# A hand-written order for the SAGE loop of a four-layer graph network, and three steps for one in the last endings

## The chip, the cores and the metric

The kernel runs on one core of a Trainium2 chip. The metric is the device time of one execution in microseconds (us); the time of a kernel is the median of its runs. Engines are named as the profile names them: PE (TensorE matmul), PEld (TensorE weight load), ACT (ScalarE), DVE (VectorE), POOL (GpSimd), SP (SyncE).

## The reference

A graph of N = 3327 nodes with an int32 adjacency matrix, 512 features a node, four layers in a row. Each layer normalises its input over the features and adds its result to that input.

```
h = layernorm(x) ;  layer 0: graph attention, 8 heads of 64; then batch norm over the nodes, relu, + x  -> x1
h = layernorm(x1);  layer 1 (SAGE): mean of the neighbours' rows of relu(h);
                    own = relu(h) @ W_self + b_self ; nb = mean @ W_nb + b_nb ;
                    relu([own, nb] @ W_comb + b_comb) + x1                       -> x2
h = relu(layernorm(x2)); layer 2: graph attention, 8 heads of 64; elu, + x2      -> x3
h = relu(layernorm(x3)); layer 3: the same with its own weights; elu, + x3       -> out
```

Graph attention projects h to W h, scores each edge (i, j) by a leaky relu of a sum of one number for i and one for j, takes the softmax over the neighbours j of i, and sums the rows of W h with it.

## The kernel before, in words

Nodes are padded to 3328, 26 blocks of 128. Edges are sparse, so the kernel works on lists. For each group of 64 destination nodes (52 groups, two to a block) it holds a list of source nodes, cut into chunks of 128; the groups have 22, 15, 13, 12, 11, 10, 9, 9, 9 chunks, then four times 8, six times 7, eleven times 6, twenty-one times 5, and 4: 359 in all. A chunk's 128 source rows are fetched by one indirect DMA that POOL issues (L1106).

**Attention** (`attend`, layers 0, 2 and 3) runs over units of three chunks: DVE makes weights (L1207, L1214), PE sums rows with them (facc, L1228). When a group's sum is complete, a generator `ending(g)` finishes it in steps (sums, rd, eight products into the block, then exp, add and store), one step for each unit that follows. `later()` advances every open ending by one step and then calls `tick()`, which does one step of some other work: the folding of SAGE's weights during layer 0, the projection of layer 3 during layer 2. Attention's loop already stands inside `tc.manual_schedule` for PE, DVE and ACT: these engines take their instructions in the order in which the program's text gives them. Outside such a block the Tile scheduler chooses the order.

**SAGE** (layer 1, in `sparse`) needs no weights from DVE. Before its loop, `own` adds each block's own part into `bn_y` (s_ps, L1387). The loop then goes over parts. A part is up to two chunks (SUNIT) of each of a block's two groups; `load(i)` casts their masks on ACT (z_mask, L1444) and has POOL gather their rows (z_rows, L1106). Both have eight tile buffers (SROWS), and parts are loaded two ahead (SAHEAD). PE adds a chunk into sage_acc (L1463), in pairs, one chunk of each group. Ahead of each pair stands `tick()`, which advances each open `ending(b, acc)` by a step and then the next layer's projection by a step. The ending of a block is, step by step: s_ag (ACT, L1402: sum times 1/degree), a_ps and aT (PE transposes L1406, ACT copy L1408), n_ps (PE, L1412, and the load of fsage_x), s_o (DVE, L1417 and L1418, and the store of x2), after which the block goes to the projection.

**The projection of the next layer** (`Following`) takes each block of x2 through ten steps or so. In `norm`: ln_j, ln_s, rs_g, rs_y on ACT (sums for the mean and the variance); a DVE step of the reciprocal root; ln_s and ln_h on ACT (L795, L796). In `rest`: p_ps and hT (PE transposes L803, ACT L806); p_sd (PE, L810) and three ACT operations on it (v_row L814 and L815, s_col L817); p_wh (PE, L823); r_full, r_half and the eight products v_row (ACT, L827) and the table's store; p_tr (PE, L831); r_row and its store (ACT, L834). One `tick` does up to two steps of the oldest block in `rest`, then one step of each block in `norm`.

```
def tick(self):
    for _ in range(min(2, len(self.ready))):
        while self.ready and next(self.ready[0]) is None:
            self.ready.pop(0)
    for g in list(self.early):
        hx = next(g)
        ...
```

After the loop the open endings are run down, `proj.drain()` finishes the projection, and a row of the mean (mean_ps, L699) closes the table; layer 2's gathers wait for it.

Of the kernel before, what the change touches and what calls it, by code (L numbers as in the profile page):

```python
# [23 lines left out]
F32 = mybir.dt.float32  # L24
# [9 lines left out]
ET = mybir.EngineType  # L34
# [4 lines left out]
P = 128  # L39
H = 8  # L40
F = 64
D = H * F
# [8 lines left out]
GB = 64  # L51
CAPS = (22, 15, 13, 12, 11, 10, 9, 9, 9) + 4 * (8,) + 6 * (7,) + 11 * (6,) + 21 * (5,) + (4,)
# [8 lines left out]
SAHEAD = 2  # L61
# [1016 lines left out]
def sparse(ctx: ExitStack, tc: tile.TileContext, t: dict, out: bass.AP, WA, ls, cs, idx, rdeg, first):  # L1078
# [5 lines left out]
    nc = tc.nc  # L1084
# [4 lines left out]
    PG = P // GB  # L1089

    def used(c):
        return min(P, N - c * P)
# [12 lines left out]
    def gather(dst, src, k):  # L1105
        nc.gpsimd.indirect_dma_start(  # L1106
            out=dst, out_offset=None, in_=src[:, :], in_offset=bass.IndirectOffsetOnAxis(ap=idx[:, k : k + 1], axis=0)
        )


    def attend(layer, table, r_dram, finish, tick=lambda: None, home=None):
# [11 lines left out]
        with tc.tile_pool(name=f"fatt{layer}", bufs=2) as ap, tc.tile_pool(  # L1123
            name=f"facc_ps{layer}", bufs=2, space=PSUM
        ) as aps, tc.manual_schedule(engines={ET.PE, ET.DVE, ET.Activation}):
            rows, rrs, rbs, accs, ends = {}, {}, {}, {}, []
# [42 lines left out]
                    del hps[b]  # L1169
                    yield from fin  # L1170

            def later():
                for e in list(ends):
                    if next(e, 0) == 0:
                        ends.remove(e)
                tick()

            for g in range(2):
# [23 lines left out]
            for i, (g, k0, n, begins, stops) in enumerate(units):  # L1202
# [11 lines left out]
                nc.vector.tensor_tensor(wt[:, :n], mx[:, :n], mk.unsqueeze(2).to_broadcast(full), ALU.mult)  # L1214
                load(i + 1)
                later()
                if begins:
                    fetch(g + 2)
                    acc = aps.tile([P, BANK], F32, name="facc", tag="acc")
# [3 lines left out]
                for k in range(n):  # L1223
                    f, l = begins and k == 0, stops and k == n - 1
                    for q in range(hq):
                        for v in range(PG):
# [5 lines left out]
                                start=(f and q == 0),  # L1232
                                stop=(l and q == hq - 1),
                            )
                if stops:
                    ends.append(ending(g))
            while ends:
                later()

    def following(lx, layer, wl, W, pb=1):  # L1240

        table = dram.tile([NP, ROW], I32, name=f"table{layer}")
        r_dram = dram.tile([ls.G, 2, H, GB], F32, name=f"r_dram{layer}")
        pp = lx.enter_context(tc.tile_pool(name=f"fproj{layer}", bufs=1))
        pps = lx.enter_context(tc.tile_pool(name=f"fproj_ps{layer}", bufs=1, space=PSUM))
        return Following(tc, cs, N, wl, W, WA, table, r_dram, pp, pps, pb)
# [24 lines left out]
    with ExitStack() as mx:  # L1271
# [48 lines left out]
        with tc.tile_pool(name="beside", bufs=1) as wp, tc.tile_pool(name="beside_ps", bufs=1, space=PSUM) as wps:  # L1320
            bg = beside(wp, wps)

            def done(c, hp, pool):
                yield
                whole.append(c)
                yield

            attend(0, *first, done, lambda: next(bg, None), y)
            for _ in bg:
                pass  # L1330
# [4 lines left out]
        proj = following(mx, 2, 1, t["L2_gnn_W"], 2)  # L1335
        gp = mx.enter_context(tc.tile_pool(name="fsage", bufs=2))
        gps = mx.enter_context(tc.tile_pool(name="fsage_ps", bufs=2, space=PSUM))
        two = [P, 2, D]
        with tc.tile_pool(name="fbn", bufs=1) as bp:
            var_ps = gps.tile([P, D], F32, name="var_ps", tag="n_ps")  # L1340
            for c in range(0, NB, 2):
# [3 lines left out]
                for i in range(2):  # L1345
                    k = used(c + i)
# [51 lines left out]
        ends = []  # L1398

        def ending(b, acc):  # L1400
            ag = gp.tile([P, D], F32, name="s_ag", tag="s_ag")
            nc.scalar.mul(ag, acc, rdeg[:, b : b + 1])  # L1402
            yield
            tp = gps.tile([P, KC, P], F32, name="a_ps", tag="a_ps")
            for kc in range(KC):
                nc.tensor.transpose(tp[:, kc, :], ag[:, kc * P : (kc + 1) * P], cs["ident"])  # L1406
            aT = gp.tile([P, KC, P], F32, name="aT", tag="aT")
            nc.scalar.copy(aT, tp)  # L1408
            yield
            ps = gps.tile([P, D], F32, name="n_ps", tag="n_ps")  # L1410
            for kc in range(KC):
                nc.tensor.matmul(ps, aT[:, kc, :], Wx[:, 1, kc, :], start=(kc == 0), stop=(kc == KC - 1))  # L1412
            xr = gp.tile([P, D], F32, name="fsage_x", tag="sage_x", bufs=3)
            nc.sync.dma_start(xr, x1[b * P : (b + 1) * P, :])
            yield
            o = gp.tile([P, D], F32, name="s_o", tag="s_o", bufs=3)
            nc.vector.tensor_tensor(o, ps, y[:, b, :], ALU.add)  # L1417
            nc.vector.scalar_tensor_tensor(o, o, 0.0, xr, ALU.max, ALU.add)  # L1418
            nc.sync.dma_start(x2[b * P : (b + 1) * P, :], o)
            proj.begin(b, o)  # L1420

        def tick():
            for e in list(ends):
                if next(e, 0) == 0:
                    ends.remove(e)
            proj.tick()


        parts = []
# [3 lines left out]
        loaded = {}  # L1433

        def load(i):
            if i >= len(parts):
                return
            zs = loaded[i] = []
            for u, kn in enumerate(parts[i][1]):
                if kn is not None:  # L1440
                    k0, n = kn
                    zt = gp.tile([P, SUNIT, D], F32, name="z_rows", tag="z_rows", bufs=SROWS)
                    mf = gp.tile([P, SUNIT, GB], F32, name="z_mask", tag="z_mask", bufs=SROWS)
                    nc.scalar.copy(mf[:, :n, :], mask[:, k0 : k0 + n, :])  # L1444
                    for k in range(n):
                        gather(zt[:, k, :], h_dram, k0 + k)
                        zs.append((k, u, k0 + k, mf[:, k, :], zt[:, k, :]))
            zs.sort(key=lambda x: x[:2])

        for i in range(SAHEAD):  # L1450
            load(i)
        for i, (b, _, begins, stops) in enumerate(parts):
            load(i + SAHEAD)
            if begins:
                acc = gps.tile([P, D], F32, name="sage_acc", tag="sage_acc")
            at = -1
            for r, u, k, m, z in loaded.pop(i):
                if r != at:
                    at = r
                    tick()  # L1460
                g = b * PG + u
                f, l = k == ls.first[g], k == ls.first[g] + CAPS[g] - 1
                nc.tensor.matmul(acc[u * GB : (u + 1) * GB, :], m, z, start=f, stop=l)  # L1463
            if stops:
                ends.append(ending(b, acc))
        while ends:
            tick()
        proj.drain()


    with ExitStack() as l3:
        at2 = proj
        proj = following(l3, 3, 2, t["L3_gnn_W"])
        attend(2, at2.table, at2.r_dram, elu_into(x2, x3, proj.begin), proj.tick)
        proj.drain()
    attend(3, proj.table, proj.r_dram, elu_into(x3, out))


def gnn_stack(tc: tile.TileContext, t: dict, out: bass.AP):
    with ExitStack() as ctx:  # L1480

        tc.nc.scalar.preload_act_table_set("natural_log_exp_and_others")
        N, NP = out.shape[0], t["x"].shape[0]
        ls = Lists(NP)
        cs = constants(ctx, tc, N)
        kp = ctx.enter_context(tc.tile_pool(name="first", bufs=1))
        ldram = ctx.enter_context(tc.tile_pool(name="first_dram", bufs=1, space=DRAM))

        table = ldram.tile([NP, ROW + NP // WB // 2], I32, name="table0")
        r_dram = ldram.tile([ls.G, 2, H, GB], F32, name="r_dram0")  # L1490
        idx = kp.tile([P, ls.n], I32, name="idx")
        rdeg = kp.tile([P, NP // P], F32, name="rdeg")
        with tc.tile_pool(name="wa1", bufs=1) as wp:
            prods = Products(tc, t, kp, wp)
            WA, ok = prods.WA, prods.ok
            with tc.tile_pool(name="fproj0", bufs=1) as pp, tc.tile_pool(name="fproj_ps0", bufs=1, space=PSUM) as pps:
                p = Projection(tc, cs, N, 0, t["x"], t["L0_gnn_W"], WA, table, r_dram, pp, pps, hb=1)
                lists(tc, t, ls, cs, N, prods, table, p, idx, rdeg)
        small = tc.nc.values_load(ok[0:1, 0:1], min_val=0, max_val=1, skip_runtime_bounds_check_because="a product of comparisons, 0 or 1")
        with tc.If(small > 0) as branch:  # L1500
            sparse(tc, t, out, WA, ls, cs, idx, rdeg, (table, r_dram))
        with branch.Else():
            general(tc, t, out)
# [60 lines left out]
```

## Time and profile before

| | us |
|---|---|
| median of 3 runs | 2963.6 |
| lowest and highest run | 2959.35, 2970.7 |
| the profiled execution, its own time | 2969.83 |
| its span in the profile | 2967.7 |
| PE, DVE, POOL, ACT busy in the span | 2177.8, 1813.4, 1384.6, 1069.6 |
| SAGE's first gather, first sage_acc, last sage_acc | 1036.8, 1044.3, 1640.3 |
| layer 2's first gather | 1671.4 |

The profile shows one execution. Times on its axis run from the span's start. Busy time is what an engine's records cover; a share of busy time over the whole span mixes stages with different limits, so the SAGE stage (some 630 us, a fifth of the span) is read by itself, from stretches of 74 us, each a fortieth of the span. The mean granted PE clock of the whole execution was 0.788 of full speed.

### The profile page before, as it was taken

The page shows a single profiled execution, that of the slowest core. Times are in us where ns is not written, and L with a number is a line of the kernel's source. Part 1 is how long each engine was busy: PE and PEld are TensorE (multiplying, and loading weights), DVE is VectorE, ACT ScalarE, POOL GpSimd, SP SyncE. Part 2 cuts the span into 40 slices and gives each one's busy share as a digit, 9 for nine tenths or more (in the row PEclk, how much of TensorE's full clock was granted, in tenths as well). Part 3 has the DMA queues.
Part 4 walks back from the last instruction along what each step waited for, and adds up shares of the span by engine and source line. Part 5 has one row for each costly group of instructions (what it writes and reads, how often), then busy time and mean ns, then how long its engine had stood idle before and what let it go on. Part 6 is the DMA issues. An engine that isn't in the chain of part 4 may idle for free.

```text
span 2967.7 us, 54270 instructions
## 1 busy us (share of the span) xinstructions
PE 2177.8 (73%) x21344; PEld 1372.4 (46%) x21344; DVE 1813.4 (61%) x2208; ACT 1069.6 (36%) x4013; POOL 1384.6 (47%) x1482
## 2 busy tenths in 40 slices
PE   2677577877675985888999567878777657677775
PEld 1444344555552431333333355655555346556664
DVE  8878487878776800011111377778667267888886
ACT  1233022323334412344455213555666501222333
POOL 1000365666550056656555365555444066666653
PEclk9778798867778997889999777877777766775655
DMA  7771477777662746666666466777565066677774
GB/s 280 279 263 56 161 233 231 252 210 213 200 200 77 249 142 194 192 203 209 198 199 189 131 184 186 202 199 195 169 177 165 31 192 190 194 199 198 205 203 127
DMA packets 188820, 562.09 MB, mean 189 GB/s; under 512 B 37780, under 2 KB 42320, under 8 KB 185230
## 3 DMA queue, kind: packets, MB, share of 16 engines
q0 software_dynamic: 115456, 404.86, 47.4%
q1 hardware_dynamic: 73102, 153.68, 14.7%
q8 instruction: 171, 2.80, 0.4%
q14 instruction: 91, 0.75, 0.1%
HBM read 498.74 MB, written 59.68 MB: 188 GB/s over the span
## 4 chain that ended last, share of the span: by engine, by line
PE 57%; issue 15%; ACT 8%; another core or an unknown queue 4%; DVE 3%; DMA 2%; POOL 0%; SPq 0%; DVEq 0%; ACTq 0%; POOLq 0%
PE facc L1228 29%; PE p_wh L823 7%; PE sage_acc L1463 5%; PE n_ps L1412 3%; PE r_bc L1139 3%; PE p_sd L810 2%; PE s_ps L1387 2%; ACT v_row L827 2%; PE bmean_ps L1315 1%; ACT fhp L1166 1%; PE fwx_ps L1305 1%; DVE mx L1207 1%; PE p_ps L803 1%; ACT hT L806 1%
## 5 line engine op out<-in xcount | busy, mean ns | idle before, releaser
L1106 POOL DMA_INDIRECT rows<-table,idx x1077 | 1025.3, 952 | 882.4 <-PE facc L1228 378.4
L1228 PE MATMUL facc<-rows,wgt 128*64 128x65 f32 x17232 | 982.1, 268 | 411.2 <-issue 399.1
L1228 PEld LDWEIGHTS facc<-rows,wgt 128*64 128x64 f32 x17232 | 829.8, 176 | 631.3 <-issue 588.1
L1207 DVE TENSOR_TENSOR mx<-r_bc,rows 128x1536 f32<-128x1536 f32 (+1 forms) x405 | 639.6, 1579 | 157.8 <-PE facc L1228 71.4
L1214 DVE TENSOR_TENSOR wgt<-mx,mask 128x1536 f32<-128x1536 f32 (+1 forms) x405 | 638.3, 1576 | 158.5 <-PE facc L1228 81.7
L1106 POOL DMA_INDIRECT z_rows<-h_dram,idx x359 | 340.2, 948 | 387.8 <-ACT hT L1384 140.2
L1166 ACT ACTIVATE fhp<-sums,rd 64x64 f32<-64x64 f32 x832 | 219.8, 334 | 137.5 <-DVE rd L1160 71.4
L1463 PE MATMUL sage_acc<-z_rows,z_mask 128*64 128x512 f32 x718 | 229.0, 655 | 9.6 <-DMA z_rows<-h_dram,idx 8.9
L823 PE MATMUL p_wh<-fWt,hT 128*128 128x512 f32 x416 | 227.1, 693 | 1.4 <-ACT s_col L817 1.4
L1156 ACT COPY sums<-facc 128x260 f32<-128x260 f32 x156 | 57.9, 371 | 402.6 <-PE facc L1228 366.3
L820 DVE TENSOR_SCALAR s_col<-s_col 128x8 f32<-128x8 f32 x52 | 9.9, 190 | 303.3 <-ACT s_col L817 125.6
L1199 ACT ACTIVATE mask<-on 128x192 uint8<-128x192 uint16 (+1 forms) x135 | 46.5, 344 | 375.3 <-DVE on L1193 214.3
L823 PEld LDWEIGHTS p_wh<-fWt,hT 128*128 128x128 f32 x416 | 89.8, 227 | 109.5 <-issue 105.0
L1027 POOL DMA_DIRECT2D list_b<-shift x12 | 6.0, 504 | 277.7 <-DVE shift L983 277.7
L827 ACT ACTIVATE v_row<-p_wh,v_row 128x64 f32<-128x64 f32 x416 | 90.7, 329 | 121.3 <-PE p_wh L823 98.3
L1417 DVE TENSOR_TENSOR s_o<-n_ps,bn_y 128x512 f32<-128x512 f32 x26 | 18.0, 691 | 184.7 <-PE n_ps L1412 139.7
L810 PE MATMUL p_sd<-WA,hT 128*128 128x16 f32 x416 | 74.7, 304 | 65.4 <-ACT hT L806 57.0
L680 PE MATMUL wh_ps<-fWt,hT 128*128 128x512 f32 x208 | 122.0, 741 | 0.0
L810 PEld LDWEIGHTS p_sd<-WA,hT 128*128 128x128 f32 x416 | 71.2, 245 | 99.1 <-ACT hT L806 68.0
L1412 PE MATMUL n_ps<-fWx,aT 128*128 128x512 f32 x208 | 106.0, 645 | 6.8 <-ACT aT L1408 6.6
L1166 ACT ACTIVATE bn_y<-sums,rd 64x64 f32<-64x64 f32 x416 | 109.5, 333 | 2.4 <-DVE rd L1160 0.5
L1463 PEld LDWEIGHTS sage_acc<-z_rows,z_mask 128*64 128x64 f32 x718 | 53.8, 145 | 114.4 <-issue 101.9
(197 smaller groups left out, 2135.8 us busy)
## 6 DMA issues: line engine op xcount, KB each, us to landing
adj_i<-in_adj SPq DMA_DIRECT2D x26, 1664.0 KB
table<-v_row SPq DMA_DIRECT2D x78, 264.0 KB
rows<-table,idx POOLq DMA_INDIRECT x1077
fin_x<-fx SPq DMA_DIRECT2D x52, 256.0 KB
ln_x<-in_x SPq DMA_DIRECT2D x26, 256.0 KB
bn_x<-in_x SPq DMA_DIRECT2D x13, 512.0 KB
fx<-bn_x SPq DMA_DIRECT2D x13, 512.0 KB
fsage_x<-fx SPq DMA_DIRECT2D x26, 256.0 KB
```

The costliest lines, as they stand in the source:

```text
L680: nc.tensor.matmul(wh, hT[:, kc, :], self.Wt[:, kc, :], start=(kc == 0), stop=(kc == KC - 1))
L810: nc.tensor.matmul(sd[:, : 2 * H], hT[:, kc, :], WA[wl][:, kc, :], start=(kc == 0), stop=(kc == KC - 1))
L823: nc.tensor.matmul(wh, hT[:, kc, :], self.Wt[:, kc, :], start=(kc == 0), stop=(kc == KC - 1))
L827: nc.scalar.mul(V[:, h, 0:F], wh[:, h * F : (h + 1) * F], V[:, h, F : F + 1])
L1106: nc.gpsimd.indirect_dma_start(out=dst, out_offset=None, in_=src[:, :], in_offset=bass.IndirectOffsetOnAxis(ap=idx[:, k : k + 1], axis=0))
L1139: nc.tensor.matmul(rb, ones[0:2, :].bitcast(F32R), rrs.pop(g).bitcast(F32R), start=True, stop=True)
L1166: nc.scalar.mul(hp[o0 : o0 + GB, h * F : (h + 1) * F], sm[mine, q, 0:F], rd[mine, q, :])
L1207: nc.vector.tensor_tensor(mx[:, :n], rbs[g].unsqueeze(1).to_broadcast(full), gt[:, :n, H * (F + 1) : ROW].unsqueeze(3).to_broadcast(full), ...
L1214: nc.vector.tensor_tensor(wt[:, :n], mx[:, :n], mk.unsqueeze(2).to_broadcast(full), ALU.mult)
L1228: nc.tensor.matmul(accs[g][v * GB : (v + 1) * GB, q * (F + 1) : (q + 1) * (F + 1)], wt[:, k, h, :], gt[:, k, h * (F + 1) : (h + 1) * (F + 1)],
L1412: nc.tensor.matmul(ps, aT[:, kc, :], Wx[:, 1, kc, :], start=(kc == 0), stop=(kc == KC - 1))
L1463: nc.tensor.matmul(acc[u * GB : (u + 1) * GB, :], m, z, start=f, stop=l)
```

## The change

Three edits, none of which adds or removes an instruction.

First, SAGE's loop, with the loads ahead of it, the running down of its endings and the draining of the projection, goes into a `manual_schedule` block for PE, DVE and ACT, as attention's loops already are. POOL and SP are not named in it.

Second, a `yield` is set between the transposes a_ps and the copy aT, so that an ending of SAGE has five steps, and aT and n_ps each come one step later.

Third, the advance of the endings is taken out of `later()` (attention) and `tick()` (SAGE) into `nearer()`, and where only endings are left (`while ends`), each round advances them three steps and the other work one, where before it was one and one. That touches layers 0, 2 and 3 as well as SAGE.

```
-            def later():
+            def nearer():
                 for e in list(ends):
                     if next(e, 0) == 0:
                         ends.remove(e)
+
+            def later():
+                nearer()
                 tick()
...
             while ends:
-                later()
+                for _ in range(3):
+                    nearer()
+                tick()
...
                 nc.tensor.transpose(tp[:, kc, :], ag[:, kc * P : (kc + 1) * P], cs["ident"])
+            yield
             aT = gp.tile([P, KC, P], F32, name="aT", tag="aT")
...
-        def tick():
+        def nearer():
             for e in list(ends):
                 if next(e, 0) == 0:
                     ends.remove(e)
+
+        def tick():
+            nearer()
             proj.tick()
...
-        for i in range(SAHEAD):
-            load(i)
-        for i, (b, _, begins, stops) in enumerate(parts):
...
+        with tc.manual_schedule(engines={ET.PE, ET.DVE, ET.Activation}):
+            for i in range(SAHEAD):
+                load(i)
+            for i, (b, _, begins, stops) in enumerate(parts):
...
-        while ends:
-            tick()
-        proj.drain()
+            while ends:
+                for _ in range(3):
+                    nearer()
+                proj.tick()
+            proj.drain()
```

The body of the loop in the block is otherwise the old one, line by line.

More of the change, by code (lines that the diff above doesn't have):

```diff
@@ L1448, in load @@
             zs.sort(key=lambda x: x[:2])
-        for i in range(SAHEAD):
-            load(i)
-        for i, (b, _, begins, stops) in enumerate(parts):
[L1453 to L1459, printed above, removed]
-                    tick()
[L1461 to L1465, printed above, removed]
-        while ends:
-            tick()
-        proj.drain()
+        with tc.manual_schedule(engines={ET.PE, ET.DVE, ET.Activation}):
+            for i in range(SAHEAD):
+                load(i)
+            for i, (b, _, begins, stops) in enumerate(parts):
+                load(i + SAHEAD)
+                if begins:
+                    acc = gps.tile([P, D], F32, name="sage_acc", tag="sage_acc")
+                at = -1
+                for r, u, k, m, z in loaded.pop(i):
+                    if r != at:
+                        at = r
+                        tick()
+                    g = b * PG + u
+                    f, l = k == ls.first[g], k == ls.first[g] + CAPS[g] - 1
+                    nc.tensor.matmul(acc[u * GB : (u + 1) * GB, :], m, z, start=f, stop=l)
+                if stops:
+                    ends.append(ending(b, acc))
+            while ends:
[3 more added lines that the diff above has]
+            proj.drain()
     with ExitStack() as l3:
```

## The prediction

> **What bounds the kernel now.** I read the page's tables of slices and groups first, to find what the SAGE stage is made of; then the stretches of busy time, to see where in it TensorE has room; then the list of waits, to see which order makes the room; last the chain of waits.
>
> ```profile
> PE   2677577877675985888999567878777657677775
> PEclk9778798867778997889999777877777766775655
> L1106 POOL DMA_INDIRECT z_rows<-h_dram,idx x359 | 340.2, 948 | 387.8 <-ACT hT L1384 140.2
> L1463 PE MATMUL sage_acc<-z_rows,z_mask 128*64 128x512 f32 x718 | 229.0, 655 | 9.6 <-DMA z_rows<-h_dram,idx 8.9
> L823 PE MATMUL p_wh<-fWt,hT 128*128 128x512 f32 x416 | 227.1, 693 | 1.4 <-ACT s_col L817 1.4
> L1412 PE MATMUL n_ps<-fWx,aT 128*128 128x512 f32 x208 | 106.0, 645 | 6.8 <-ACT aT L1408 6.6
> ```
>
> One slice is 74 us. The SAGE stage runs from the first z_rows gather at 1036.8 us to the first gather of layer 2 at 1671.4, slices 15 to 22: TensorE starts it at 5 to 8 tenths and ends it at 9, with the clock rising with it. 359 gathers are all that GpSimd does there.
>
> ```profile
> core 0: us, PE busy (x) PEld busy (x) DVE busy (x) ACT busy (x) POOL busy (x), PEclk, DMA share, GB/s
> 1113.00:1187.00 74.00, 43.18 (x131) 14.78 (x131) 4.27 (x12) 17.43 (x67) 46.56 (x51) 0.77 0.66 194
> 1187.00:1261.00 74.00, 60.24 (x183) 23.16 (x184) 5.13 (x16) 26.43 (x115) 44.72 (x48) 0.87 0.64 192
> 1261.00:1335.00 74.00, 62.98 (x210) 24.02 (x210) 8.28 (x24) 31.13 (x133) 43.29 (x47) 0.88 0.66 202
> 1335.00:1409.00 74.00, 62.12 (x209) 24.78 (x206) 7.51 (x25) 32.45 (x140) 47.23 (x50) 0.95 0.67 210
> 1409.00:1483.00 74.00, 67.89 (x225) 27.11 (x225) 9.68 (x27) 36.02 (x151) 40.91 (x45) 0.95 0.64 198
> 1557.00:1631.00 74.00, 68.56 (x244) 27.69 (x243) 9.65 (x31) 42.48 (x180) 39.22 (x41) 0.98 0.63 192
> ```
>
> No engine but TensorE is near full: in the last stretch it works 68.6 of 74 us, in the first 43.2, and no other passes 47. What holds it in the first half are waits:
>
> ```profile
> PE a_ps L1406 <- ACT s_ag L1402: 15.5, 5, 13.2
> PE p_sd L810 <- ACT hT L806: 10.6, 1, 10.6
> PE p_tr L831 <- DVE r_half L740: 8.9, 4, 4.1
> PE p_ps L803 <- ACT ln_h L796: 7.7, 4, 4.4
> PE n_ps L1412 <- ACT aT L1408: 6.6, 2, 4.8
> PE sage_acc L1463 <- DMA z_rows<-h_dram,idx: 5.2, 3, 1.8
> ...
> ACT v_row L814 <- remote: 29.2, 4, 10.0
> ACT z_mask L1444 <- PE sage_acc L1463: 29.4, 19, 6.4
> ACT z_mask L1444 <- remote: 19.1, 3, 9.1
> ```
>
> These are 1113 to 1631 us: total wait, times, longest. Of 84.6 us only 5.2 are for gathered rows; the rest is ScalarE's and VectorE's answers. They are few and long: s_ag once 13.2, hT once 10.6. ScalarE is late because it stands itself: a z_mask cast waits 8.8 us until 1117.3, then s_ag another 9.4 of its own; a cast waits 9.2 until 1184.2 with hT queued behind it, and TensorE stops for want of that hT.
>
> The chain of waits over 1044 to 1700 names "another core or an unknown queue" for 11.5%, some 75 us. There is no other core. I put it to semaphores that arrive long after the record of the work: p_sd is recorded done at 1316.6 and its exps start at 1327.2.
>
> [...] So what an order puts ahead of a late wait matters. [...] the eight p_wh passes take 3.53 us in the busy stretches and 6.36 at 1656, after idling.
>
> **The change, part by part.** No instruction is added or removed. GpSimd's order is the same; SyncE's differs in six places, each a store or load with a neighbour. I cost these at nothing: each store is wanted only by the next layer, and fsage_x is ready long before its s_o, which waits for n_ps (130.3 us in all on VectorE).
>
> *The SAGE loop by hand.* Before, the scheduler places single matmuls (one p_sd, one sage_acc pair, three p_sd) and hoists z_mask casts. After, each step has one pair of sage_acc matmuls, then whole groups, and a cast stands two parts ahead of use, behind the work of the steps before. Worked from rows: a sage pair takes 0.97 us of TensorE, start to start; a block takes n_ps 3.53, p_wh 3.63, p_sd 0.93, a_ps 0.6, p_ps 0.6, p_tr 0.21, together 9.5. A block with 5, 6 or 7 pairs so needs 14.35, 15.3 or 16.3 us.
>
> What the written order leaves of waits, for two blocks: p_ps waits for ln_h, since the eight v_row products (1.75 us) stand ahead of ln_s and ln_h on ScalarE: 1.4. p_sd follows p_ps at once and waits for hT: 1.7. a_ps waits for s_ag behind products (1.75) and the ln_j chain (2.4), less the sage pairs that cover it: 2.5. Sum 5.6 for two blocks, 2.8 each. ScalarE has 42 of 74 us of work and isn't the bound; a wait on it (exps for p_sd, aT for a_ps) now holds z_mask casts only two parts from use.
>
> - Blocks 0 to 5 (s_ag from 1127.1 to 1268.1): the gathers, 1.25 us start to start, allow block 5 at about 1231, so at most 37 us. If the hT stand behind a cast (10.6) goes and the s_ag stand (13.2, a late semaphore of its own) stays: **-10** (0 to -37).
> - Blocks 5 to 11 (n_ps 1277.3 to 1405.8, 21.4 us a block): 41 pairs and 6 x 9.5 make 96.8, 16.1 a block; with 2.8 that is 18.9, so -15. Gathers allow 16.7. Half stays, as the late semaphores come with any order: **-8** (0 to -20).
> - Blocks 11 to 24 (1405.8 to 1630.1, 17.25 a block): 68 pairs and 13 x 9.5 make 189.5, 14.6 a block; with 2.8 that is 17.4: **+2** (-15 to +35; see the rival).
> - GpSimd's waits for TensorE (68 us behind sage_acc, 46 behind p_tr) shrink with TensorE's; no price of their own.
>
> *The additional step between a_ps and aT.* One sage pair (0.97) covers a_ps' way to ScalarE and back, where n_ps waited 6.6 us in all. An ending gets one step of about 3 us longer, and still fits in the next block's five. The accumulator is free after s_ag, as before. Nothing of its own.
>
> *Three steps for one at ends.* The last ending of SAGE is a chain of dependent work already (s_ag 1640.9, n_ps 1643.1, p_wh 1656.1, end 1670): 0 to -2. Layer 0's is covered by ScalarE's products of bn_y: 0. In layer 2's, after the last facc at 2309.5, 4.6 to 5.0 us of ending work stand twice between one block's products and the next p_ps; drawn together they overlap: 0 to -9. Layer 3 has no projection behind it: 0. Together **-4**.
>
> Sum: -10 - 8 + 2 - 4 = -20. Against the profiled execution (2969.8; its span 2967.7, 2 us lie around it) that is 2950. It ran 6.2 above the median of the three runs, so I say 2944 for the median.
>
> **The rivals.**
>
> *B, the waits change their names only.* If late semaphores come with long trains of gathers and not with the order, stages 0 to 11 stay as they are and the tails give 4: 2958 to 2962. For it: GpSimd's order is untouched, and the stands end 1 to 2.5 us after GpSimd stops (1124.4 and 1127.0; 1325.3 and 1327.9). Against it: the stand at 1184 holds TensorE only through what is queued behind the cast.
>
> *C, slower: the in-order ScalarE stream.* The scheduler did ln_j and ln_h during p_wh, ahead of the products, and could fill a wait with single matmuls; a written order can do neither. If the three waits (5.6 us) come in each block rather than in each second one, blocks 11 to 24 take 14.6 + 5.6 = 20.2 against 17.25: +38; blocks 5 to 11 take 21.7 against 21.4: +2. With -10 early and -4 at the ends this is +26, or 2990 against the median. With w us of waits a block, half the gain of blocks 5 to 11 kept, the change is worth 3(w - 5.3) + 13(w - 2.65) - 14: nothing at w = 4.0, and 14.8 slower at 4.9. There it decides. For it: ScalarE rises to 42 of 74 us late, where the cycles of before are good (14.4 to 15.7 us at best). Against it: the best are few, 17.25 is their mean.
>
> *A, the whole room is won:* -37 - 20 - 15 - 11 = -83, 2881. Against it: it needs every stand gone, the late semaphores' too.
>
> *D, the order isn't what the text says.* Excluded for TensorE: after the change groups of four are whole between pairs. Not excluded that it differs little in the loops of attention, where only the ends move.
>
> **How the numbers follow.** A measurement can tell about 0.5% from no change here, 14.8 us: 2948.8 and 2978.4. My forecast with A: 0.43, nearly all beyond the lower bound though close to it. B and half-gains: 0.27. C: 0.30. The likeliest is 2944; its own range is 2906 to 2958. For eight in ten I keep B and most of C: 2906 to 2991.
>
> **What would show it.** Right: s_ag of block 5 by 1258 or earlier; ScalarE's z_mask waits below 20 us of the 48.5; 19 to 20 us a block up to block 11; about 17.4 after it; the first gather of layer 2 near 1655; from there everything shifted unchanged up to layer 2's end. B: z_mask or v_row L814 waits of 9 us stay, block 5 near 1268. C: a_ps on s_ag and p_ps on ln_h at 1.4 us and over in most blocks, 20 us a block late. The forecast is wrong if the gap between the two kernels' first gathers of layer 2 isn't the gap of the whole, within the 4 us of the ends.

## The result and the profile after

The changed kernel takes 2980.2 us (median of 20 runs, 2962.6 to 2991.0), the kernel before 2965.4 in 20 runs beside it (2959.4 to 2974.1): a ratio of 1.0040, 95% interval 1.0027 to 1.0052. I had said 2944. The profiled execution of after has a span of 2979.8 us, 12.1 more than before's.

The runs fell on chips of two kinds, and no number below can be understood without that. The two traces named before and after are from A (before 2965 us) and a second group is from B (before 3007 us). All other runs fell on C, which stands for four chips (11, 12, 13 and 15 in the record) where before takes 2593 to 2595 us. Ratios are always to before on the same chip. Traces of C are compared across its four chips; the stretch that matters most below, blocks 18 to 25, agrees there for one and the same kernel (118.1, 118.0 and 118.0 us for e_fill on chips 12, 15 and 13).

These are the lines of after's page (slices and groups) that answer to those of before:

```profile
PE   3677577777775976888889567877777656777775
PEclk9778788977777997899998778878777767776656
L1106 POOL DMA_INDIRECT z_rows<-h_dram,idx x359 | 340.2, 948 | 389.0 <-ACT hT L1389 140.4
L823 PE MATMUL p_wh<-fWt,hT 128*128 128x512 f32 x416 | 229.0, 701 | 1.7 <-ACT s_col L817 1.4
L1474 PE MATMUL sage_acc<-z_rows,z_mask 128*64 128x512 f32 x718 | 210.8, 667 | 8.5 <-DMA z_rows<-h_dram,idx 7.6
L1418 PE MATMUL n_ps<-fWx,aT 128*128 128x512 f32 x208 | 112.1, 688 | 8.8 <-ACT aT L1414 7.8
```

The counts of these groups are the same. sage_acc is busy 18 us less (210.8 for 229.0), yet n_ps takes 688 ns a pass (one matmul record) for 645. The same stretches of time as for before:

```profile
core 0: us, PE busy (x) PEld busy (x) DVE busy (x) ACT busy (x) POOL busy (x), PEclk, DMA share, GB/s
1113.00:1187.00 74.00, 45.97 (x141) 17.02 (x141) 4.77 (x14) 19.19 (x79) 47.27 (x51) 0.74 0.65 195
1187.00:1261.00 74.00, 61.92 (x183) 22.50 (x183) 5.99 (x16) 24.12 (x102) 43.31 (x47) 0.82 0.63 192
1261.00:1335.00 74.00, 63.22 (x224) 25.15 (x221) 7.44 (x25) 35.02 (x145) 47.20 (x50) 0.91 0.69 211
1335.00:1409.00 74.00, 61.54 (x206) 23.88 (x207) 8.49 (x25) 32.71 (x139) 45.24 (x48) 0.95 0.65 203
1409.00:1483.00 74.00, 65.63 (x234) 26.46 (x230) 9.59 (x31) 38.74 (x164) 43.36 (x47) 0.95 0.67 214
1557.00:1631.00 74.00, 67.10 (x208) 27.09 (x208) 9.00 (x28) 34.97 (x153) 33.38 (x36) 0.86 0.55 170
```

The last row says it: TensorE is as busy as before (67.1 for 68.6), but with 208 matmul records for 244, at a granted clock of 0.86 for 0.98. Busy time isn't work here. The waits of TensorE and ScalarE, 1113 to 1640 us (total, times, longest):

```profile
PE a_ps L1411 <- ACT s_ag L1407: 21.8, 8, 13.2
PE p_sd L810 <- ACT hT L806: 12.6, 5, 10.2
PE p_ps L803 <- ACT ln_h L796: 8.9, 7, 2.0
PE a_ps L1411 <- ACT z_mask L1453: 8.5, 5, 1.9
...
ACT hT L806 <- remote: 23.1, 3, 14.5
ACT s_ag L1407 <- remote: 19.8, 2, 18.5
ACT z_mask L1453 <- PE sage_acc L1474: 0.4, 1, 0.4
```

The casts no longer wait (48.5 us before), as forecast. But hT and s_ag wait themselves for what I read as late semaphores (`remote`, 23.1 and 19.8 us), and TensorE stands for them as long as before (13.2 us for s_ag, 10.2 for hT). In the late blocks, short waits of 0.6 to 1.9 us have come. In the timeline of after (start, duration, work, and in brackets the idle time before it) one such place:

```profile
1553.88 1.08 PE L1474 MATMUL sage_acc<-z_rows,z_mask 128*64 128x512 f32 x4
1556.06 0.66 PE L803 MATMUL p_ps<-fident,ln_h 128*128 128x128 f32 x4 [1.11 <-ACT ln_h L796]
1557.34 1.53 PE L810 MATMUL p_sd<-WA,hT 128*128 128x16 f32 x8 [0.62 <-ACT hT L806]
1558.81 1.98 PE L1474 MATMUL sage_acc<-z_rows,z_mask 128*64 128x512 f32 x4
1560.71 5.66 PE L1418 MATMUL n_ps<-fWx,aT 128*128 128x512 f32 x8
1566.21 3.60 PE L823 MATMUL p_wh<-fWt,hT 128*128 128x512 f32 x8
...
1574.76 0.99 PE L1411 MATMUL a_ps<-fident,s_ag 128*128 128x128 f32 x4 [1.87 <-ACT z_mask L1453]
1575.68 1.98 PE L1474 MATMUL sage_acc<-z_rows,z_mask 128*64 128x512 f32 x4
```

After 1.11 and 0.62 us of idling, p_sd takes 1.53 for 0.96, a sage pair's group 1.98 for 1.08, n_ps 5.66 for 3.70: some 3.5 us lost behind 1.7 us of waits, until p_wh takes 3.60 us again (3.68 at 1646.74 in before), at a clock of 1.00. The granted clock of that place, in stretches cut where it changes:

```profile
1554.46:1557.87 3.41, 1.68 (x13) 0.95 (x9) 0.00 (x0) 3.38 (x17) 2.50 (x4) 1.00 0.80 238
1557.87:1564.70 6.83, 6.83 (x15) 3.04 (x15) 0.28 (x1) 1.40 (x9) 3.33 (x4) 0.50 0.69 217
1564.70:1574.94 10.24, 8.37 (x27) 2.85 (x26) 2.05 (x6) 4.96 (x20) 2.94 (x4) 1.00 0.38 116
1574.94:1578.35 3.41, 3.41 (x12) 1.42 (x11) 0.00 (x0) 1.78 (x5) 2.73 (x3) 0.50 0.72 223
```

The first row has TensorE busy for 1.68 of its 3.41 us; the clock is halved in the next (0.50 for 1.00).

Where the time went, from the starts of s_ag and of the gathers (us, one trace each; c_ends_only has the loop in before's order, its only part of the change being the last endings):

| | A before | A after | B before (b_again) | B after (a_again) | C c_ends_only | C after (a_third) |
|---|---|---|---|---|---|---|
| first gather to s_ag of block 0 | 90.3 | 90.3 | 91.8 | 92.1 | 65.8 | 66.1 |
| blocks 0 to 5 | 141.0 | 141.5 | 147.1 | 141.5 | 122.5 | 123.5 |
| blocks 5 to 11 | 131.6 | 125.8 | 130.6 | 126.0 | 108.3 | 107.7 |
| blocks 11 to 18 | 126.3 | 122.4 | 131.6 | 132.6 | 111.6 | 117.8 |
| blocks 18 to 25 | 114.9 | 133.2 | 116.5 | 131.3 | 102.5 | 125.8 |
| last s_ag to layer 2's first gather | 30.5 | 36.8 | 30.5 | 35.6 | 30.1 | 34.5 |
| layer 2's last gather to layer 3's first | 75.9 | 75.8 | 75.7 | 75.6 | 77.8 | 77.8 |

On A the loop gains 9 us up to block 18, loses 18 in the next seven blocks and 6 at SAGE's end. Layers 2 and 3 give and take under 2. Blocks 18 to 25 of before and of after, on A:

```profile
1526.00:1640.93 114.93, 106.64 (x365) 43.28 (x365) 15.92 (x49) 63.35 (x270) 56.86 (x60) 0.97 0.60 185
1515.45:1648.66 133.21, 117.15 (x365) 47.58 (x365) 15.67 (x50) 64.39 (x278) 55.08 (x59) 0.87 0.51 162
```

The same 365 matmul records are busy 10.5 us longer at a clock of 0.87 for 0.97, and 7.8 us of idle time are added. On B it is the other way round: of 14.8 us, 10.9 are idle time and 4.0 busy time (clock 0.91 for 0.95).

My theory from here: in the late blocks TensorE is nearly full, so each wait of the written order is added to the end, and its clock falls after them, which costs as much again. The rivals: the additional step or the endings alone make the loss; or it is the waits alone, the clock a companion; or the late semaphores make the late waits too.

### The profile page after: what moved, and what is told of

Read it like the earlier page. It is cut to its first block, busy times and chain, and to the rows that moved or that the text cites. A ratio compares the mean times of both kernels' runs of the same rounds, so it can differ in the third digit from the quotient of the medians.

```text
span 2979.8 us, 54265 instructions
## 1 busy us (share of the span) xinstructions
PE 2172.4 (73%) x21344; PEld 1371.2 (46%) x21344; DVE 1812.6 (61%) x2208; ACT 1067.9 (36%) x4013; POOL 1383.3 (46%) x1482
## 3 DMA queue, kind: packets, MB, share of 16 engines
q0 software_dynamic: 115456, 404.86, 46.7%
q1 hardware_dynamic: 73102, 153.68, 14.7%
## 4 chain that ended last, share of the span: by engine, by line
PE 56%; issue 16%; ACT 9%; another core or an unknown queue 3%; DVE 2%; DMA 2%; POOL 1%; SPq 0%; DVEq 0%; ACTq 0%; POOLq 0%
PE facc L1231 29%; PE p_wh L823 7%; PE sage_acc L1474 4%; PE n_ps L1418 3%; PE r_bc L1139 2%; PE p_sd L810 2%; PE s_ps L1392 2%; ACT v_row L827 2%; PE bmean_ps L1320 1%; PE fwx_ps L1310 1%; ACT fhp L1166 1%; DMA rows<-table,idx 1%; PE p_ps L803 1%; ACT hT L806 1%
## 5 line engine op out<-in xcount | busy, mean ns | idle before, releaser
L823 PE MATMUL p_wh<-fWt,hT 128*128 128x512 f32 x416 | 229.0, 701 | 1.7 <-ACT s_col L817 1.4
L1474 PE MATMUL sage_acc<-z_rows,z_mask 128*64 128x512 f32 x718 | 210.8, 667 | 8.5 <-DMA z_rows<-h_dram,idx 7.6
L820 DVE TENSOR_SCALAR s_col<-s_col 128x8 f32<-128x8 f32 x52 | 9.5, 183 | 268.7 <-ACT s_col L817 126.9
L827 ACT ACTIVATE v_row<-p_wh,v_row 128x64 f32<-128x64 f32 x416 | 90.8, 330 | 170.5 <-PE p_wh L823 155.3
L1418 PE MATMUL n_ps<-fWx,aT 128*128 128x512 f32 x208 | 112.1, 688 | 8.8 <-ACT aT L1414 7.8
L1139 PE MATMUL r_bc<-r_two,fones 2*128 2x512 f32 x156 | 95.4, 615 | 14.3 <-issue 6.7
```

Source lines behind the costliest of these rows:

```text
L823: nc.tensor.matmul(wh, hT[:, kc, :], self.Wt[:, kc, :], start=(kc == 0), stop=(kc == KC - 1))
L827: nc.scalar.mul(V[:, h, 0:F], wh[:, h * F : (h + 1) * F], V[:, h, F : F + 1])
L1139: nc.tensor.matmul(rb, ones[0:2, :].bitcast(F32R), rrs.pop(g).bitcast(F32R), start=True, stop=True)
```

## The experiments

**The parts of the change.** m1_manual_only is before with the loop in the manual block, nothing else:

```
+        with tc.manual_schedule(engines={ET.PE, ET.DVE, ET.Activation}):
             for i in range(SAHEAD):
...
             while ends:
                 nearer()
                 proj.tick()
```

> The SAGE loop in manual order, with no additional step before aT and the old endings. Theory (waits in ScalarE's written order, and TensorE's clock halved after them, cost the late blocks): from s_ag of block 18 to s_ag of block 25 it takes 128 to 138 us, as after (133.2; before 114.9), and the whole is 5 to 15 us slower than before. Rival (the additional step lengthens each ending and makes the loss): 115 to 120 us there, and 5 us or more faster than before, since blocks 5 to 18 keep their 9.6 us. End of SAGE, last s_ag to layer 2's first gather: near 30.5 as before if the three-for-one endings made it 36.8, near 36 if the order or the clock did.

c_ends_only is before with three `nearer()` for one `tick()` in both `while ends` loops:

> Three steps for one in the last endings alone; the SAGE loop stays with the scheduler. Theory: nothing measurable, within 3 us of before; layer 2's end, last gather to layer 3's first, stays at 75.8 us, since ScalarE's ending work is only moved from one wait to another. My forecast was -4. Rival (the three-for-one endings cost SAGE's end 6 us): 4 to 8 us slower than before, all between the last s_ag and layer 2's first gather.

Both ran on C: m1_manual_only 2611.6 us, ratio 1.0078 (1.0057 to 1.0100); c_ends_only 1.0001 (0.9992 to 1.0009). The latter is as expected in the whole. But layer 2's end, from its last gather to layer 3's first, takes 77.8 us there and 74.4 in m1_manual_only. All 14 traces of C agree: 77.8 (five) or 75.6 (two) with the new endings, 74.4 (five) or 75.7 (two) with the old. So on C the new endings make it no shorter, and mostly 3 us longer. To compare with after, b_again (before), a_again (after) and m2_manual_yield were run, the last being after with this undone:

```
             while ends:
-                for _ in range(3):
-                    nearer()
-                tick()
+                later()
...
-                for _ in range(3):
-                    nearer()
+                nearer()
                 proj.tick()
```

> The kernel before, for a trace beside the other runs of this group. On the chip of the last group (before: 2595 us there), block 18 to block 25 should take some 102.5 us with TensorE busy all the time, as in c_ends_only; on the chip of the first traces 114.9.

> The changed kernel, for its traces beside the others on one chip. Theory (TensorE has little room late, so each wait of the written order is added to the end): slower than before by 15 to 40 us where the chip leaves before without waits late (2595 us kind), by 10 to 15 us on the first kind. Rival (the loss belongs to the first chip's clock): no slower than before where the clock is not reduced.

> The change without its third part: manual order and the additional step, old endings. If the endings of three steps cost time, this is 4 to 10 us faster than a_again, all of it between the last s_ag and layer 2's first gather and at layer 2's end; if they cost nothing, it is within 3 us of it. Against m1_manual_only (ratio 1.0078 to before) it tells what the additional step does: theory, nothing to 5 us worse, since aT's way to TensorE was no long wait late.

They fell on B: a_again 1.0014 (1.0003 to 1.0024), less of a loss than expected; m2_manual_yield 1.0003 (0.9989 to 1.0017); b_again one run, 3004.0. From the last s_ag to layer 2's first gather m2_manual_yield takes 31.0 us for 35.6 in a_again: the three-for-one endings cost SAGE's end 4.6 us in the written order (by one trace each; the medians of the two are only 1.1 us apart), while blocks 18 to 25 stay at 131.7. Then after itself on C:

> The changed kernel beside the others of this group. On a 2595 us kind of chip: theory, 0.6 to 1.0% slower than before, as m1_manual_only, as before has no room late there (102.5 us for blocks 18 to 25, TensorE always busy) and after's waits are added in full, 110 to 114 us. On a 3000 us kind: 0.1 to 0.4% slower, as twice before.

2642.1 us, ratio 1.0193 (1.0157 to 1.0230), twice the loss expected. Stretches of block 18 to block 25 on C, of c_ends_only, m1_manual_only (both chip 12) and a_third (chip 13), columns as above:

```profile
1351.90:1454.40 102.50, 102.44 (x370) 42.47 (x366) 15.99 (x49) 63.04 (x269) 56.71 (x60) 1.00 0.68 208
```

```profile
1355.50:1467.30 111.80, 103.06 (x370) 42.52 (x369) 15.08 (x47) 63.17 (x268) 57.00 (x61) 0.98 0.62 192
```

```profile
1360.70:1486.50 125.80, 111.15 (x369) 44.66 (x365) 15.69 (x48) 64.19 (x276) 55.79 (x59) 0.92 0.52 167
```

On C the order of before has no room in the late blocks: TensorE is busy 102.44 of 102.50 us. The manual block adds 9.3, nearly all of it idle time (8.7). After's other parts add 14.0: 5.9 of idle time and 8.1 of busy time for the same matmuls, the clock going from 0.98 to 0.92. The endings aren't in this stretch, so that is the additional step. It lengthens the waits. All of TensorE's in this stretch, of m1_manual_only, then of a_third (total, times, longest):

```profile
PE a_ps L1409 <- ACT s_ag L1405: 4.2, 3, 1.4
PE p_sd L810 <- ACT hT L806: 1.8, 4, 0.5
PE p_ps L803 <- ACT ln_h L796: 1.6, 3, 0.5
```

```profile
PE a_ps L1411 <- ACT s_ag L1407: 5.6, 3, 1.9
PE p_ps L803 <- ACT ln_h L796: 4.4, 4, 1.1
PE p_sd L810 <- ACT hT L806: 2.3, 4, 0.6
```

**The clock.** e_fill is after with dummy matmuls in the waits of the odd blocks from 13 on. The edit at a_ps; p_ps and p_sd get one each:

```
             tp = gps.tile([P, KC, P], F32, name="a_ps", tag="a_ps")
+            if b % 2 and b >= 13:
+                for _ in range(2):
+                    nc.tensor.matmul(tp.rearrange("p k c -> p (k c)"), cs["ident"], proj.Wt[:, 0, :], start=True, stop=True)
             for kc in range(KC):
```

> After, with dummy matmuls (bits of the weights times the identity, into tiles that the real work overwrites) put before a_ps (two), p_ps (one) and p_sd (one) of the odd blocks from 13 on, where TensorE waits 1.9, 1.1 and 0.6 us: 3.5 us of added work for each pair of blocks. Theory of the clock: the waits stay but TensorE isn't idle, the clock in that stretch goes from 0.87 to over 0.93, n_ps goes from 5.4-5.9 us to 3.7, and block 18 to block 25 takes 122 to 128 us in place of 133.2, added work and all. Rival (the waits alone cost the time, the clock is a companion): 133 to 137 us and no gain.

> e_fill again (after, with dummy matmuls before the three waits of the odd blocks from 13 on), for a 3000 us kind of chip. Theory of the clock: block 18 to 25 takes 122 to 128 us in place of 131 to 133, though 14 us of dummy work lie in it, and the clock there is over 0.93. Rival (waits alone): 133 us or more, the clock no matter.

> The changed kernel with dummy matmuls in its waits. On a 3000 us kind of chip: theory of the clock, 122 to 128 us for blocks 18 to 25 in place of 131 to 133, clock over 0.93, n_ps 3.7 us in each block; rival (waits alone), 133 us or more. On a 2595 us kind: 118 us as twice before, and beside a_third it tells what the fillers cost where the clock holds.

All three ran on C: ratios to before 1.0133 (1.0118 to 1.0148), 1.0131 (1.0106 to 1.0156) and 1.0137 (1.0097 to 1.0176; two runs, on a_third's chip). Block 18 to 25 takes 118.0 us in each; e_fill_3:

```profile
1360.20:1478.20 118.00, 116.21 (x401) 46.71 (x397) 15.55 (x48) 64.00 (x277) 55.80 (x59) 1.00 0.56 179
```

With 13.8 us more matmuls in it than c_ends_only's 102.4, the stretch is 7.8 us shorter than a_third's. The whole is some 12 us shorter by the medians (2630.2 for 2642.1), though with two and four runs the intervals of the two ratios still touch. Idle time falls from 14.7 to 1.8, the clock is 1.00. Here filling the waits costs nothing by itself; what it saves is the half clock. The rival of waits alone is out: of a_third's 23.3 us over c_ends_only, 14.6 are idle time and 8.7 busy time at the slower clock. That the lowered clock costs time is shown on C, by this edit; for A and B it is read from the records (0.87 for 0.97; 0.91 for 0.95).

**What the waits come from.** h_dve is after with the eight products of a block of SAGE's projection in one operation on VectorE (in the code, `self.pb == 2` picks out the projection that runs in SAGE):

```
-        for h in range(H):
-            nc.scalar.mul(V[:, h, 0:F], wh[:, h * F : (h + 1) * F], V[:, h, F : F + 1])
+        if self.pb == 2:
+            nc.vector.tensor_tensor(
+                V[:, :, 0:F], wh.rearrange("p (h f) -> p h f", f=F), V[:, :, F : F + 1].to_broadcast([P, H, F]), ALU.mult
+            )
+        else:
+            ...
```

That operation takes 0.69 us on VectorE (v_row L827 in hb_dve_3), for the 1.74 of ScalarE's eight (L827 at 1328.25 in before). h2_dve_old_ends has the old endings besides; hb_dve_before is before with this edit alone.

> After, with the eight products v_row of a block done by VectorE in one operation (SAGE's projection only); VectorE is busy 8 to 10 of 74 us there. Theory (the products ahead of ln_h and of the ln_j chain on ScalarE make p_ps and a_ps wait): both waits go, 1.75 us of ScalarE a block becomes some 0.7 of VectorE, the clock stays up, and block 18 to block 25 takes 101 to 110 us; the whole is 20 to 35 us faster than after. Rival (the waits come from late semaphores, not from what stands ahead): within 5 us of after.

> h_dve again (after, with the products of SAGE's projection on VectorE), hoping for a chip on which before takes 2965 to 3007 us, since on the 2595 us kind before had no waits to lose late. Theory (the products ahead of ln_h and s_ag on ScalarE make the late waits of the written order, and the clock falls behind them): block 18 to 25 falls from 131-133 us to 103-112, the clock there from 0.87 to over 0.95, and the whole is 20 to 30 us faster than after. Rival (late semaphores make the late waits): 125 us and more there. On the 2595 us kind: again within 0.5% of before.

> Manual order, the additional step, VectorE's products, and the old endings. On a 3000 us kind of chip SAGE's end, from the last s_ag to layer 2's first gather, should take 27 to 31 us where h_dve_2 takes 31 to 36; all else as h_dve_2; so 3 to 6 us faster than it, and 0.8 to 1.2% faster than before. If the endings don't matter, equal to h_dve_2.

> Manual order, the additional step, products on VectorE, old endings. On a 3000 us kind of chip: theory, blocks 18 to 25 fall from 131-133 us to 103-112 with the clock at 0.95 and more, and the whole is 0.8 to 1.3% faster than before. Rival (late semaphores make the late waits): 125 us and more there, within 0.4% of before. On a 2595 us kind: within 0.2% of before, as h2_dve_old_ends.

All on C: h_dve 1.0024 (1.0015 to 1.0033) and 1.0024 (1.0016 to 1.0032); h2 1.0007 (0.9997 to 1.0016) and 1.0001 (0.9991 to 1.0012). Block 18 to 25 of h2_dve_2, and all the waits of its TensorE there:

```profile
1348.80:1452.10 103.30, 101.25 (x370) 41.79 (x366) 20.34 (x59) 52.10 (x213) 55.80 (x59) 1.00 0.64 207
```

```profile
PE p_sd L810 <- ACT hT L806: 1.8, 4, 0.5
```

The waits for s_ag and ln_h are gone, the clock is whole: 103.3 for a_third's 125.8. On C the late loss comes of the products in ScalarE's written order. The edit also takes work from ScalarE (52.1 us for 64.2), but ScalarE was far from full (64.2 of 125.8 us), so I put it to what stands behind the products; a kernel that leaves them on ScalarE in a later place wasn't tried. That h_dve doesn't beat before on C was said beforehand only for the second pair of runs. The first expectation (20 to 35 us faster than after) is passed: by the ratios, 1.0024 against 1.0193 in different groups, it is some 44 us; beside a_third, h2_dve_2 is 46.7 us faster (2595.4 for 2642.1). No run of h_dve fell on A or B, so the same is not shown for them; that their late waits are nearly as long (1.9, 1.1 and 1.0 us at most on A) only speaks for it.

> The kernel before with only the products v_row of SAGE's projection moved to VectorE (one operation a block for ScalarE's eight). Theory (late, TensorE is the bound where the clock holds; early, the gathers are): nothing late on a 2595 us kind of chip, -5 to -15 us on the first kind, where waits of before remain. Rival (ScalarE's queue holds the early blocks): 10 us and more on either.

> The kernel before with SAGE's products on VectorE, as hb_dve_before. On a 2595 us kind of chip: within 0.3% of before, as TensorE is busy all the time in blocks 18 to 25 and the gathers set the pace of blocks 0 to 5. On a 3000 us kind: 0.5 to 0.9% faster again.

On B hb_dve_before is the best of its group: 2980.4 us, 0.9925 (0.9904 to 0.9946), beyond the gain expected. Its gain there is up to block 18 (138.7, 126.9 and 122.7 us for b_again's 147.1, 130.6 and 131.6); blocks 18 to 25 got slower (120.7 for 116.5), so late waits aren't what it saves on B. On C the ratio is 0.9957 (0.9942 to 0.9971), where I expected no more than 0.3%. The gain on C is mostly in blocks 11 to 18, 103.0 us for 111.6, for a reason told at the end, and in blocks 5 to 11 (104.0 for 108.3). So before with the products on VectorE beats both kernels, on B and on C.

**The early blocks.** n_few_gathers is before with the gathers of blocks 0 to 5 left out but for the first eight tiles, which are added again (their sums are other numbers).

```
+                    again = parts[i][0] <= 5 and len(held) == SROWS
+                    if again:
+                        zt = held[(2 * i + u) % SROWS]
...
+                        if not again:
                             gather(zt[:, k, :], h_dram, k0 + k)
```

> Before, without the gathers of blocks 0 to 5 but for the first eight tiles: later parts of these blocks add the same eight tiles again, so the sums of these blocks are other numbers. Theory (PE's semaphores come late while GpSimd issues long trains of gathers; that holds s_ag of block 0 and hT): on a 3000 us kind of chip the first gather to s_ag of block 0 falls from 90 to some 66 us, block 0 to 5 from 141-147 to 100-112, and no wait of 9 us is left there. Rival (the late semaphores have to do with TensorE's own stream or the clock): the waits of 9 to 13 us stay with few gathers, and block 0 to 5 stays over 125.

> Before, with the gathers of blocks 0 to 5 left out but for the first eight tiles, which are added again in their place. On a 3000 us kind of chip: theory (semaphores of TensorE come late in trains of gathers), first gather to s_ag of block 0 some 66 us in place of 90, blocks 0 to 5 100 to 112 in place of 141 to 147. Rival (they have to do with TensorE itself): the waits of 9 us and more stay. On a 2595 us kind: as n_few_gathers.

> Before, with the gathers of blocks 0 to 5 left out but for the first eight tiles, which are added again in their place. On a 3000 us kind of chip: theory (semaphores of TensorE come late in trains of gathers), first gather to s_ag of block 0 58 to 66 us in place of 90, blocks 0 to 5 92 to 112 in place of 141 to 147. Rival (late for TensorE's own reasons): the waits of 9 us and more stay. On a 2595 us kind: 58 and 91.5 again.

All three fell on C, one run each: blocks 0 to 5 take 91.5 us each time for 122.5, with TensorE idle for 0.2 us of them where it was 16.1, and the whole takes 2550 to 2556 us. On C the gathers set the early pace: 97 of them from block 1 to block 5 at before's 1.25 us, start to start, are 121. Whether the late semaphores of A and B come from the gathers stays open, since no run without the gathers fell there.

## Why the prediction was wrong, point by point

- *Blocks 0 to 5, -10.* Measured +0.5 on A (-5.6 on B). The step that failed: that TensorE stood at 1184 only because hT was queued behind a cast. The cast is gone from its way, and hT still waits for a late semaphore, with TensorE standing for 10.2 us. Rival B had these blocks right (block 5 at 1267.2, forecast near 1268). Why the semaphores come late stays open.
- *Blocks 5 to 11, -8.* -5.8 on A (-7.0 between the n_ps starts that the prediction used), -4.6 on B: right in size, the mechanism only in part. On A 3.3 us are idle time (19.6 for 22.9); the rest is busy time, in which sage_acc falls from 51.8 to 44.3 us, a gain that I hadn't priced. On C nothing is won (107.7 for 108.3).
- *Blocks 11 to 24, +2.* This is the term that decided: +14.3 on A from block 11 to 25 (-3.9 up to block 18, +18.3 after it), +15.9 on B. The waits are there and no longer than forecast: I had 5.6 us of idling for two blocks, after shows 4.6 on A (16.05 in seven blocks) and 4.2 on C (14.65). The step that failed is the price of the work, 14.35 us a block at full clock, with nothing for a clock that the waits lower. On A two blocks should so take 28.7 + 4.6 = 33.3, and take 38.1. Most of the other 4.8 is the clock; some 0.6 is a price set too low, for on C at clock 1.00 two blocks are busy 29.3 (102.4 in seven). I had seen p_wh take 6.36 us for 3.53 after idling and put no price on it for my own, shorter waits; in after a clock of 0.50 follows waits of 1.11 and 0.62 us close together. My own example should have told me: the slow p_wh at 1656 comes after waits of 2.81 and 0.46 us, at a clock of 0.50 from 1654.81 to 1661.64. On A blocks 18 to 25 take 19.0 us each, where 17.4 was forecast (blocks 11 to 18 do take 17.5): 18.3 more than before, of which 7.8 are idle time (16.1 for 8.3) and 10.5 are matmuls at a lower clock (117.2 busy for 106.6). I also took the mean of before's later blocks, 17.25, for all: its last seven run at 16.4, so there was less to win. And the gain up to block 18 has its own unpriced part: TensorE is idle 5.0 us more there (13.7 for 8.7) and busy 8.9 us less (108.7 for 117.6), since sage_acc runs in pairs (told at the end).
- *The additional step, nothing of its own.* The step that failed on C: that one sage pair covers it. It costs 14 us in blocks 18 to 25. I had costed its own latency, but the waits for s_ag and ln_h grow (1.9 and 1.1 us for 1.4 and 0.5); that it shifts s_ag, the products and ln_h against each other is my reading. On A and B it wasn't tried alone.
- *Ends, -4.* SAGE's end +6.4 on A and +5.1 on B; 4.6 of the latter goes with the old endings. The step that failed: that a chain of dependent work can't get slower. Three steps at once put the last block's n_ps ahead of the p_ps of the block before. On A that n_ps starts at 1650.7, on a clock of 0.54 after waits of 2.8 and 0.6 us, and takes 6.74 us; p_ps comes only at 1657.3, and its hT behind ln_j. Layer 2's end: 0 on A and B, since ScalarE's ending work only moved, from two waits of TensorE (3.5 and 4.3 us) to one of 5.8 and one of 5.3; on C as told above.
- *The sum* on A: +0.5 - 5.8 + 14.3 + 6.4 is +15.4 for the SAGE stage, where -20 was forecast with the ends; what lies outside gave back 3.3, which makes the 12.1 of the two traces.
- *Rival C*, slower by ScalarE's in-order stream, was the right mechanism, as far as C shows it; I had given it 0.30. Its price was not right: the waits come in every second block, 2.3 us of idling a block on A, below its deciding 4.0; the clock made up the rest.
- *The test named beforehand*, that layer 2's first gather shows the whole difference within the 4 us of the ends, holds: 14.1 us there, 12.1 in all.

## What to carry to other kernels

Where TensorE is nearly full (93% busy in the late blocks on A, all of the time on C), price twice a wait that an order brings in: its length, and the slower matmuls behind it until the clock is back (14.6 and 8.7 us of a_third's 23.3 in blocks 18 to 25 on C). Before ordering by hand, list for each engine what a short, urgent operation (s_ag, ln_h) stands behind in its own stream; here moving the long work to an engine with room (VectorE, busy for 20.3 of 103.3 us in h2_dve_2) was worth more than the order. And read a profile's waits as those of its chip: the late idle time of before is 8.3 us on A and none on C.

## What was not expected of the hardware

- The same program takes 2593 to 2595 us on four chips and 2965 to 3007 on others; why isn't known. From the first gather to block 0's s_ag it takes 66 us in c_ends_only (C) for 90 in before (A). A gather of z_rows takes nearly the same on GpSimd: 948 ns in before (A), 948 in b_again (B: 53.11 us busy for 56 in blocks 18 to 25) and 945 in c_ends_only (C: 56.71 for 60).
- Two sage_acc matmuls, one for each half of the partitions of the sum, run side by side when they follow each other: their records start 6 or 7 ns apart in before and after, and the four passes take 1.08 us (1553.88 in after). Two passes alone take 1.07, as in this line of before's timeline:

```profile
1527.38 1.07 PE L1463 MATMUL sage_acc<-z_rows,z_mask 128*64 128x512 f32 x2
```

The scheduler's order splits many pairs, the written one few: from block 0's s_ag to block 25's, 122 of 640 passes start with no other beside them in before, and 18 in after. That goes with the 18 us by which sage_acc is busy less in after. On C hb_dve_3 takes 40.7 us for the 154 passes of blocks 11 to 18 (8 of them alone) that take 48.9 in c_ends_only (some 39 alone), which is most of its 8.6 us there.
- In after, waits of 1.11 and 0.62 us with p_ps' 0.66 between them are followed by half the clock for 6.83 us, and one of 1.87 by half for 3.41 (the rows at 1557.87 and 1574.94). In the traces of before and after each record of the granted clock says 1.00 or 0.50, and the shortest stretch from change to change in the SAGE stage is 3.41 us. I divided that stage of both, from block 0's s_ag to block 25's, into stretches of this length, with the changes on their borders. Of those at a clock of 1.00 with TensorE idle for less than 45% of them, 1 of 206 is followed by one at 0.50; of those with 55% and more, 20 of 22; in between, 10 of 12. So in these two traces the half clock follows the stretches with much idle time, whether in two waits (1.73 us in the one from 1554.46) or in one (1.87 in the one before 1574.94); why it falls, they don't show. It fits that m1_manual_only, with waits of 1.4 us at most in blocks 18 to 25, keeps a clock of 0.98 there, and a_third, with waits of 1.9 and of 1.1 and 0.6, has 0.92.
